# A decoder layer's FFN on one core: the inner layernorm moved behind the second product, its root on GpSimd

## The chip, the core and the metric

The kernel runs on one core of a Trainium2 chip. The core has a matrix engine (TensorE, PE in the profile, with its weight loads shown as PEld), a vector engine (VectorE, DVE), an activation engine (ScalarE, ACT), a general engine (GpSimd, POOL) and a queue engine that issues most DMAs here (SyncE, SP). Each engine works through its own queue in order and waits on semaphores for the others. The metric is the device time of one launch in microseconds. The kernel before took 1366.59 us, the median of three runs (1365.82 to 1367.46).

## The reference

One decoder layer on x of shape (4, 1024, 256): self-attention of 16 heads, cross-attention to 64 context rows, and an FFN with an inner layernorm and ternary weights. Each of the three is added to x.

```python
x = x + attn(layernorm(x), ...)          # 16 heads of 16, 1024 keys
x = x + xattn(layernorm(x), ctx, ...)    # 16 heads of 16, 64 keys
x = x + ffn(layernorm(x), W_fc, ln_w, ln_b, W_proj)

def ffn(x, W_fc, ln_w, ln_b, W_proj):    # 256 -> 1024 -> 256
    h = einsum('btd,hd->bth', x, absmean(W_fc))      # absmean: -1, 0 or 1
    h = gelu(h)
    mu = mean(h, -1); var = mean((h - mu) ** 2, -1)
    h = (h - mu) * rsqrt(var + 1e-5) * ln_w + ln_b
    return einsum('bth,dh->btd', h, absmean(W_proj))
```

The inner layernorm is over the 1024 hidden columns of each token. Its mean and its root are numbers per token, ln_w and ln_b are numbers per hidden column.

## The kernel before

The tokens are worked in four batches of 1024; x lies in three slots of SBUF (`x_slots`) and goes to DRAM and back between the stages (`x_kept`). The program has two parts.

*Attention.* A loop over 16 units (a batch and a group of four heads) runs scores, exponentials and the weighing with v. Generators hang beside it in lines (`due`, `later`, `aside`): the next batch's first layernorm and projections, the batch before's output rows (`post`: the output projection of the self-attention, and the whole cross-attention), and in the last batch the making of the ternary weights (`ternary`) and of one row, `yrow`. That row is the product of ln_b with W_proj; `bias_row` has GpSimd spread ln_b over 128 columns (L764) and TensorE multiply it by the weights in strips of 32 columns, 32 matmuls, and DVE copies the result.

*The last stretch.* What is left when the attention ends is the FFN for all four batches, in eight halves of 512 tokens, and the last batch's `post`. PSUM is divided anew: two tiles of two banks (`wide`) and four of one bank (`misc`). For each half there are two generators.

- `widen(i)`: normalises four token tiles of x (`xn`, DVE, L256), transposes them on TensorE, copies them as a high part `xh` (ScalarE, L269) and a low part `xl` (DVE, L271), has GpSimd add `yrow` to x (L280), and then for each of the four token tiles multiplies by W_fc (eight matmuls of 512 columns: high and low part, two blocks of the width 256, two halves of the 1024 columns), takes Gelu on ScalarE into `h` (L1001) and the statistics on DVE (`bn_stats` L1004, `bn_aggr` L1005). When all four are there, it takes the root on ScalarE (`ln_rstd`: Sqrt L239, reciprocal on DVE L240), the shift `nmr` (DVE L1009), and normalises `h` in place, two tiles on DVE (L1012) and two on ScalarE (L1015).
- `narrow(i)`: for each of the eight blocks c of 128 hidden columns transposes the four token tiles of `h` on TensorE (L60), copies the result times ln_w as a high part `hT` (ScalarE, L1035) and a low part `hl` (DVE, L1036), and two blocks later multiplies both by W_proj into one `wide` tile `py`. At the end DVE adds `py` to x, two token tiles at a time (L1052), and SyncE writes them out.

The order of the work is written by hand. Each generator is cut into pieces by its `yield`s: `widen` into nine, `narrow` into nine. `WIDE` and `NARROW` give each piece a place on a common line of 16 places a half, and the loop at the end takes the piece with the lowest place. Two of every five turns go to a piece of `post` (`turn % 5 in (0, 2)`). A half's Gelu and Sqrt pieces are held back while `post` is between its exponentials (`apart`), and the last two halves wait until `post` is done (`late_x`), since they read its rows. TensorE's and SyncE's instructions keep this order; on the other engines a scheduler orders the instructions as it expects them to be ready, and each engine then keeps to that order.

The bank holds: a `misc` tile is free again when its readers are done; `py` holds one of the two `wide` tiles through a `narrow`, so that a W_fc tile has to wait for the Gelu of the one before it.

Of the kernel before, what the change touches and what calls it, by code (L numbers as in the profile page):

```python
# [8 lines left out]

F32 = mybir.dt.float32  # L10
F32R = mybir.dt.float32r
DRAM = bass.MemoryType.DRAM
AF = mybir.ActivationFunctionType
ALU = mybir.AluOpType
# [6 lines left out]
HID = 1024  # L21
P = 128
# [8 lines left out]
def decoder_layer(ctx, tc, a, out):  # L31
# [151 lines left out]
    def bank():  # L183
        return ps[state["banks"]]()
# [51 lines left out]
    def ln_rstd(pool, rs, mv):  # L236
        n = mv.shape[1]
        sd = pool.tile([P, n], F32, tag="sd", name="sd", bufs=2)
        nc.scalar.activation(sd, mv[:, :, 1], AF.Sqrt, bias=eps_t[:, 0:1])  # L239
        nc.vector.reciprocal(out=rs, in_=sd)  # L240

    def ln_normalised(pool, mv, rs, i, t, n):
        xn = pool.tile([P, n, E], F32, tag="xn", name="xn", bufs=2)
# [473 lines left out]

    ternaries = []

    yrow = const.tile([P, E], F32, name="yrow")  # L720

    def ternary(name, *shape):

# [33 lines left out]
                ALU.is_gt, ALU.subtract,  # L757
            )

    def bias_row():  # L760

        yield "free"
        wide = main.tile([P, HID // P, P], F32, tag="hl", name="lnb_wide", bufs=2)
        nc.gpsimd.tensor_copy(  # L764
            wide, late["lnb"].rearrange("p (c o) -> p c o", o=1).to_broadcast([P, HID // P, P])
        )
        yield "cols"
        pt = bank()
        w = ternaries[1].bitcast(F32)
        product(pt[:, 0:E], [(wide[:, c, :], w[:, c, :]) for c in range(HID // P)])  # L770
        nc.vector.tensor_copy(yrow, pt[:, 0:E])

    def run(gen):
        for _ in gen:
# [116 lines left out]
    for u in range(NU):  # L891
        b, g = divmod(u, NG)
        due.end = aside.end = 2 * NT * NG * (b + 1)
        later.end = due.end - 2
        if b % 2 and g == 0:
            due.end = 2 * NT * (u + 1)
        if g == 0:
            if b == 0:
                later.add(context(), 6)
                later.add(value_bias(), 1)  # L900

            for n in ((1, 2), (), (3,), ())[b]:
                if n > 1:
                    load_x(n)
                due.add(ln1(n), 2)
                due.add(project(n, 0), 8)
                due.add(values(n), 8)
                if n == 1:
                    due.add(project(n, 1), 8)
            if b % 2:  # L910

                due.add(project(b // 2 + 2, 1), 8)
            if b == B - 1:
                load_x(0, view=x_kept, slot=1)
        if g == 1 and b == B - 1:
            aside.add(ternary("wfc", 2, HID), 10)
            aside.add(ternary("wproj", HID // P, E), 10)
            aside.add(bias_row(), 2)
        for step in range(2 * NT):
            half, kb = divmod(step, NT)  # L920
            if step < 2 and u + 1 < NU:
                if step == 0:
                    while pieces_of.get(divmod((u + 1) // 2, NG // 2)) != 4:
                        due.step()
                    fetching = fetch(u + 1)
                next(fetching)
            next(loading, None)
            due.grow(2 * NT * u + step)
            later.grow(2 * NT * u + step)
            aside.grow(2 * NT * u + step)  # L930
            exps = [scores(u, half, kb, 0)]
            top()
            behind = 1 if later.credit >= 1.5 else 0
            if turning and begun[turning[0]] < slots[0]:
                fill("rows", behind)
                run(turning.popleft())
            elif urgent:
                fill("rows", behind)
                urgent.popleft()()
            else:  # L940
                fill("rows", 1)
            exps.append(scores(u, half, kb, 1))

            for _ in range(2 if u == 0 and step < 3 else 1):
                top()
            if pending is not None:
                if pending[2] == 0:
                    acc = ps["acc"]()
                weigh(*pending, acc)
            fill("cols", 2)  # L950
            pending = (u, half, kb, exps)
        if g == NG - 1:

            due.flush()
            aside.flush()
            later.flush()
# [13 lines left out]
    wfc, wproj = ternaries  # L970
    ffn = ctx.enter_context(tc.tile_pool(name="ffn", bufs=1))
    out_view = out.rearrange("(t p) d -> p t d", p=P)
    h_of = {}
    NH = NT // 2

    def widen(i):
        t0 = i * NH
        xh = ffn.tile([P, 2, NH * P], F32R, tag="xh", name="xh", bufs=2)
        xl = ffn.tile([P, 2, NH * P], F32R, tag="xl", name="xl", bufs=2)
        for t in range(0, NH, 2):  # L980
            cols = slice(t * P, (t + 2) * P)
            xn = ln_normalised(ffn, mv3, rs3, t0 + t, t0 + t, 2)
            ln_transposed(xh[:, :, cols], xn, rest=xl[:, :, cols])
            add_row(t0 + t, yrow)
            if t == 0:
                yield ""
        h = ffn.tile([P, NH, HID], F32, tag="h", name="h", bufs=2)
        mv = ffn.tile([P, NH, 2], F32, tag="mvh", name="mvh", bufs=2)
        rs = ffn.tile([P, NH], F32, tag="rsh", name="rsh", bufs=2)
        h_of[i] = h  # L990
        for t in range(NH):
            yield "Gelu"
            ph = ps["wide"]()
            for half in range(2):
                for k in range(4):
                    c, part = divmod(k, 2)
                    matmul(
                        ph[:, half, :], lhsT=(xl, xh)[part][:, c, t * P : (t + 1) * P],
                        rhs=wfc[:, c, half * 512 : (half + 1) * 512], start=k == 0, stop=k == 3,
                    )  # L1000
            nc.scalar.activation(h[:, t, :], ph.rearrange("p a f -> p (a f)"), AF.Gelu)  # L1001
            st = ffn.tile([P, 2, 6], F32, tag="bnh", name="bnh", bufs=3)
            for half in range(2):
                nc.vector.bn_stats(out=st[:, half, :], in_=h[:, t, half * 512 : (half + 1) * 512])  # L1004
            nc.vector.bn_aggr(out=mv[:, t, :], in_=st)  # L1005
        yield "Sqrt"
        ln_rstd(ffn, rs, mv)
        nmr = ffn.tile([P, NH], F32, tag="nmr", name="nmr", bufs=2)
        nc.vector.scalar_tensor_tensor(nmr, mv[:, :, 0], -1.0, rs, ALU.mult, ALU.mult)  # L1009
        for t in range(0, NH, 2):  # L1010
            yield ""
            nc.vector.tensor_scalar(  # L1012
                h[:, t, :], h[:, t, :], mv[:, t, 0:1], rs[:, t : t + 1], ALU.subtract, ALU.mult
            )
            nc.scalar.activation(  # L1015
                h[:, t + 1, :], h[:, t + 1, :], AF.Identity, bias=nmr[:, t + 1 : t + 2],
                scale=rs[:, t + 1 : t + 2],
            )

    def narrow(i):  # L1020


        h = h_of.pop(i)
        t0 = i * NH
        py = ps["wide"]()
        parts = []
        for c in range(HID // P + 2):
# [10 lines left out]
            if c >= 2:  # L1038
                for k, part in enumerate(parts[c - 2]):
                    for n in range(NH):  # L1040


                        matmul(
                            py[:, n // 2, n % 2 * E : (n % 2 + 1) * E], lhsT=part[:, n * P : (n + 1) * P],
                            rhs=wproj[:, c - 2, :], start=c == 2 and k == 0 and n % 2 == 0,
                            stop=c == HID // P + 1 and k == 1 and n % 2 == 1,
                        )
            if 0 < c < HID // P + 1:
                yield ""
        for n in range(2):  # L1050
            rows = xs(t0 + 2 * n, 2)
            nc.vector.tensor_tensor(  # L1052
                rows, rows, py[:, n, :].rearrange("p (n d) -> p n d", n=2), ALU.add
            )
            dma(out=out_view[:, t0 + 2 * n : t0 + 2 * n + 2, :], in_=rows)
        if i == 1:
            load_x(2, view=x_kept, slot=1)

# [15 lines left out]

    WIDE, NARROW = (-6, -4, 0, 1, 3, 7, 8, 10, 12), (2, 4, 5, 6, 9, 11, 13, 14, 15)
    halves = 2 * B
    wides = [Source(widen(i), 16 * i, WIDE) for i in range(halves)]
    narrows = [Source(narrow(i), 16 * (i + 1), NARROW) for i in range(halves)]  # L1080
# [1 line left out]
    tag = later.tag  # L1082
    while tag is not None or narrows:
        turn += 1
        if tag is not None and turn % 5 in (0, 2):
            exps += "Exp" in tag
            tag = next(last, None)
            continue
        sources = []
        if wides:  # L1090
            i = halves - len(wides)
            first = len(wides[0].places) <= len(WIDE) - 2
            late_x = i >= 2 * (B - 1) and tag is not None
            full = first and len(narrows) > halves + 1 - i
            apart = exps % NG and tag is not None and wides[0].tag in ("Gelu", "Sqrt")
            if not (late_x or full or apart):
                sources.append(wides[0])
        if narrows and len(narrows) > len(wides):
# [65 lines left out]
```

## Time and profile before

| what | value |
|---|---|
| median of three runs | 1366.59 us |
| the profiled execution | 1365.17 us |
| its span, first to last instruction | 1363.4 us |
| mean granted TensorE clock | 0.979 |
| TensorE busy in the span | 1282.1 us, 94% |
| VectorE busy | 1004.7 us, 74% |
| ScalarE busy | 898.5 us, 66% |
| GpSimd busy | 80.0 us, 6% |

The last stretch begins at 1102.5 us of the span. At 1281 the last matmul of `post` has run, and from there to 1358.5 TensorE has the FFN alone.

How to read it: a row of a group names the line, the engine, the operation, the tile written and the tiles read, the shapes, the count, then the busy time in all and the mean duration in ns, and behind the bar the idle time of the engine just before and what ended it. The chain of waits is followed back from the last instruction: each piece is the work that the next one waited for. In the busy time by stretch each engine's busy microseconds stand with the count of its instructions, and the granted clock as a share of full speed. A plain matmul on 32-bit floats shows as two records.

### The profile page before, as it was taken

How to read it: one execution, taken by the hardware profiler on the slowest of the kernel's cores; microseconds unless marked ns; L12 is line 12 of the kernel's file. 1: busy time of each engine (PE TensorE's matmuls, PEld its weight loads, DVE VectorE, ACT ScalarE, POOL GpSimd, SP SyncE). 2: the span in 40 equal slices, each digit the busy share in tenths (PEclk: the TensorE clock that was granted, in tenths of full speed). 3: DMA queues.
4: the chain of work that ended last, by engine and by line, in shares of the span. 5: the costliest groups of instructions: out<-in, count | busy, mean ns of one | idle time of the engine just before them, and what ended most of it. 6: DMA issues, size and time to landing. Idle time of an engine off the chain costs nothing.

```text
span 1363.4 us, 27651 instructions
## 1 busy us (share of the span) xinstructions
PE 1282.1 (94%) x11000; PEld 717.4 (53%) x11000; DVE 1004.7 (74%) x2110; ACT 898.5 (66%) x1654; POOL 80.0 (6%) x86
## 2 busy tenths in 40 slices
PE   3879999999999999999999999999999988999987
PEld 1434445545545454444545544545455466776777
DVE  4877777867878877877877777878889357565665
ACT  1377666756687667777676676676766746474765
POOL 4000000003010000011000000010000012000000
PEclk9889999999999999989999999999999989999989
DMA  5440312312130202131212112212210010100000
GB/s 169 126 143 30 111 42 68 94 48 63 41 85 1 63 7 57 33 93 31 64 35 60 38 27 75 82 53 73 55 40 1 2 62 1 44 19 31 1 31 32
DMA packets 46064, 72.72 MB, mean 53 GB/s; under 512 B 11280, under 2 KB 27920, under 8 KB 45936
## 3 DMA queue, kind: packets, MB, share of 16 engines
q1 hardware_dynamic: 44720, 68.47, 17.0%
q8 instruction: 87, 1.43, 0.4%
q10 hardware_dynamic: 1072, 2.10, 0.4%
q0 software_dynamic: 144, 0.39, 0.2%
q14 instruction: 41, 0.34, 0.1%
HBM read 46.81 MB, written 24.12 MB: 52 GB/s over the span
## 4 chain that ended last, share of the span: by engine, by line
PE 73%; DVE 16%; ACT 8%; issue 2%; DMA 1%; SPq 0%; DVEq 0%; ACTq 0%
PE ps_ring L57 42%; PE ps_acc L57 15%; PE ps_wide L57 8%; DVE mx L433 8%; PE ps_misc L57 3%; ACT exp L888 3%; PE ps_misc L60 2%; PE ps_ring L60 2%; DVE nm L592 2%; ACT xn L250 1%; DVE xn L256 1%; DVE bn L233 1%; DMA x<-in_x 1%; ACT ex L625 1%; ACT hl L359 1%
## 5 line engine op out<-in xcount | busy, mean ns | idle before, releaser
L433 DVE TENSOR_REDUCE mx<-ps_ring 128x1 f32<-128x512 f32 x1024 | 646.4, 682 | 157.6 <-PE ps_ring L57 156.7
L888 ACT ACTIVATE exp<-ps_ring 128x512 f32<-128x512 f32 x1024 | 549.2, 606 | 191.1 <-PE ps_ring L57 187.5
L57 PE MATMUL ps_ring<-q,k 64*128 64x512 f32 x1024 | 280.5, 474 | 8.0 <-ACT exp L888 5.9
L57 PE MATMUL ps_ring<-k,q 64*128 64x512 f32 x1024 | 260.2, 425 | 20.1 <-DMA q<-kept_q 7.9
L57 PE MATMUL ps_acc<-exp,v_sb 128*32 128x512 f32 x2048 | 275.3, 610 | 0.0
L57 PE MATMUL ps_ring<-mT,sel 64*128 64x512 f32 x1024 | 232.8, 400 | 0.2 <-ACT mT L451 0.2
L57 PEld LDWEIGHTS ps_ring<-q,k 64*128 64x128 f32 x1024 | 115.5, 185 | 198.4 <-ACT exp L888 69.0
L57 PEld LDWEIGHTS ps_ring<-k,q 64*128 64x128 f32 x1024 | 124.2, 186 | 100.2 <-ACT exp L888 41.3
L57 PEld LDWEIGHTS ps_ring<-mT,sel 64*128 64x128 f32 x1024 | 108.0, 186 | 6.3 <-ACT mT L451 0.7
L57 PEld LDWEIGHTS ps_acc<-exp,v_sb 128*32 128x32 f32 x2048 | 40.5, 108 | 67.4 <-issue 65.6
L1004 DVE BATCH_NORM_STATS2 bnh<-h 128x6 f32<-128x512 f32 x64 | 41.2, 679 | 34.1 <-ACT h L1001 34.0
L1001 ACT ACTIVATE h<-ps_wide 128x1024 f32<-128x1024 f32 x32 | 32.7, 1026 | 41.6 <-PE ps_wide L57 41.5
L1036 DVE SCALAR_TENSOR_TENSOR hl<-ps_misc,lnw,hT 128x512 fp32r<-128x512 f32 x64 | 46.4, 733 | 18.2 <-ACT hT L1035 18.2
L57 PE MATMUL ps_wide<-wproj,hl 128*128 128x256 f32 x256 | 46.2, 303 | 12.6 <-DVE hl L1036 12.5
L57 PE MATMUL ps_wide<-wfc,xl 128*128 128x512 f32 x128 | 56.5, 442 | 1.4 <-DVE xl L271 1.4
L57 PE MATMUL ps_wide<-wfc,xh 128*128 128x512 f32 x128 | 54.3, 424 | 0.0
L1035 ACT ACTIVATE hT<-ps_misc,lnw 128x512 fp32r<-128x512 f32 x64 | 42.6, 687 | 16.3 <-PE ps_misc L60 16.3
L233 DVE BATCH_NORM_STATS2 bn<-x 128x6 f32<-128x256 f32 x96 | 38.8, 416 | 8.1 <-DMA x<-in_x 6.4
L57 PEld LDWEIGHTS ps_wide<-wproj,hl 128*128 128x128 f32 x256 | 34.9, 191 | 16.2 <-DVE hl L1036 14.8
L280 POOL TENSOR_TENSOR x<-x,xbo 128x512 f32<-128x512 f32 x16 | 20.6, 1295 | 367.0 <-ACT xn L250 358.5
L57 PE MATMUL ps_wide<-wproj,hT 128*128 128x256 f32 x256 | 41.4, 284 | 0.0
L407 ACT COPY v_sb<-ps_ring 128x256 f32<-128x256 f32 x32 | 12.0, 375 | 41.0 <-PE ps_ring L57 30.6
(166 smaller groups left out, 1467.1 us busy)
## 6 DMA issues: line engine op xcount, KB each, us to landing
k<-kept_k SPq DMA_DIRECT2D x248, 64.0 KB
q<-kept_q SPq DMA_DIRECT2D x240, 64.0 KB
kept_q<-hl SPq DMA_DIRECT2D x15, 512.0 KB
kept_k<-hl SPq DMA_DIRECT2D x14, 512.0 KB
out<-x SPq DMA_DIRECT2D x16, 256.0 KB
x<-in_x SPq DMA_DIRECT2D x3, 1024.0 KB
x_kept<-x SPq DMA_DIRECT2D x3, 1024.0 KB
x<-x_kept SPq DMA_DIRECT2D x3, 1024.0 KB
```

Of the source, the lines that this page charges most:

```text
L57: ordered(nc.tensor.matmul(*args, **kwargs))
L60: ordered(nc.tensor.transpose(*args))
L233: nc.vector.bn_stats(out=st, in_=xs(t)[:, 0, :])
L250: nc.scalar.activation(xn[:, k, :], xs(t + k)[:, 0, :], AF.Identity, bias=nmr[:, k : k + 1], scale=rs[:, i + k : i + k + 1],)
L280: nc.gpsimd.tensor_tensor(xs(t, 2), xs(t, 2), row.rearrange("p (o d) -> p o d", o=1).to_broadcast([P, 2, E]), ALU.add,)
L433: nc.vector.tensor_reduce(mx[:, t, 2 * pair + n : 2 * pair + n + 1, kh], pm, AX.X, ALU.max)
L592: nc.vector.tensor_reduce(nm[:, t, s, :], pm[s].rearrange("p (h k) -> p h k", k=SK), AX.X, ALU.max, negate=True,)
L888: nc.scalar.activation(ex[:, n, :], pe[n], AF.Exp)
L1001: nc.scalar.activation(h[:, t, :], ph.rearrange("p a f -> p (a f)"), AF.Gelu)
L1004: nc.vector.bn_stats(out=st[:, half, :], in_=h[:, t, half * 512 : (half + 1) * 512])
L1035: nc.scalar.activation(hT, pt, AF.Copy, scale=w)
L1036: nc.vector.scalar_tensor_tensor(hl, pt, w, hT.bitcast(F32), ALU.mult, ALU.subtract)
```

## The change

The inner layernorm is taken through the second product. With r the root and m the mean of a token, (h - m) r ln_w W_proj is r (h ln_w W_proj) - m r (ln_w W_proj). So `narrow` multiplies `h` as it comes from Gelu, and the rest is done on the result's rows:

- `widen` no longer normalises `h`; it ends with the fourth token tile, and has six pieces instead of nine. The root and the shift -m r come from a new function, `ln_root`, on GpSimd: 17 small instructions on 128x4 numbers, a first guess from the bits of the number and three steps of Newton's method.
- A second row, `crow`, the product of ln_w with W_proj, is made as `yrow` is (`rows_of_proj` replaces `bias_row`).
- `narrow` adds crow times the shift to each of the four token tiles of x while it runs, at its blocks 4 and 6 (DVE, 128x256 each), and at its end multiplies `py` by the root and adds it to x, one token tile at a time (four DVE instructions instead of two).
- The places change, and four of every nine turns go to `post`.

```diff
+    def ln_root(pool, rs, mv):
+        n = mv.shape[1]
+        by = pool.tile([P, 4, n], F32, tag="root", name="root", bufs=2)
+        var, half, t, nmr = (by[:, i, :] for i in range(4))
+        engine = nc.gpsimd
+        engine.tensor_scalar(var, mv[:, :, 1], LN_EPS, None, ALU.add)
+        engine.tensor_scalar(half, var, -0.5, None, ALU.mult)
+        engine.tensor_scalar(
+            rs.bitcast(I32), var.bitcast(I32), -0.5, float(0x5F3759DF), ALU.mult, ALU.add
+        )
+        for _ in range(3):
+            engine.tensor_tensor(t, rs, half, ALU.mult)
+            engine.tensor_tensor(t, t, rs, ALU.mult)
+            engine.tensor_scalar(t, t, 1.5, None, ALU.add)
+            engine.tensor_tensor(rs, rs, t, ALU.mult)
+        engine.tensor_tensor(nmr, mv[:, :, 0], rs, ALU.mult)
+        engine.tensor_scalar(nmr, nmr, -1.0, None, ALU.mult)
+        return nmr
...
-    def bias_row():
+    def rows_of_proj():
+        for row, name in ((yrow, "lnb"), (crow, "lnw")):
+            yield "free"
+            wide = main.tile([P, HID // P, P], F32, tag="hl", name=f"{name}_wide", bufs=2)
+            nc.gpsimd.tensor_copy(
+                wide, late[name].rearrange("p (c o) -> p c o", o=1).to_broadcast([P, HID // P, P])
+            )
+            yield "cols"
+            pt = bank()
+            w = ternaries[1].bitcast(F32)
+            product(pt[:, 0:E], [(wide[:, c, :], w[:, c, :]) for c in range(HID // P)])
+            nc.vector.tensor_copy(row, pt[:, 0:E])
...
-            aside.add(bias_row(), 2)
+            aside.add(rows_of_proj(), 4)
...
-        yield "Sqrt"
-        ln_rstd(ffn, rs, mv)
-        nmr = ffn.tile([P, NH], F32, tag="nmr", name="nmr", bufs=2)
-        nc.vector.scalar_tensor_tensor(nmr, mv[:, :, 0], -1.0, rs, ALU.mult, ALU.mult)
-        for t in range(0, NH, 2):
-            yield ""
-            nc.vector.tensor_scalar(
-                h[:, t, :], h[:, t, :], mv[:, t, 0:1], rs[:, t : t + 1], ALU.subtract, ALU.mult
-            )
-            nc.scalar.activation(
-                h[:, t + 1, :], h[:, t + 1, :], AF.Identity, bias=nmr[:, t + 1 : t + 2],
-                scale=rs[:, t + 1 : t + 2],
-            )
+        shift_of[i] = rs, ln_root(ffn, rs, mv)
...
+            if c in (4, 6):
+                for n in range(c - 4, c - 2):
+                    row = xs(t0 + n)[:, 0, :]
+                    nc.vector.scalar_tensor_tensor(row, crow, nmr[:, n : n + 1], row, ALU.mult, ALU.add)
...
-        for n in range(2):
-            rows = xs(t0 + 2 * n, 2)
-            nc.vector.tensor_tensor(
-                rows, rows, py[:, n, :].rearrange("p (n d) -> p n d", n=2), ALU.add
-            )
-            dma(out=out_view[:, t0 + 2 * n : t0 + 2 * n + 2, :], in_=rows)
+        for n in range(NH):
+            row = xs(t0 + n)[:, 0, :]
+            nc.vector.scalar_tensor_tensor(
+                row, py[:, n // 2, n % 2 * E : (n % 2 + 1) * E], rs[:, n : n + 1], row, ALU.mult,
+                ALU.add,
+            )
+            if n % 2:
+                dma(out=out_view[:, t0 + n - 1 : t0 + n + 1, :], in_=xs(t0 + n - 1, 2))
...
-    WIDE, NARROW = (-6, -4, 0, 1, 3, 7, 8, 10, 12), (2, 4, 5, 6, 9, 11, 13, 14, 15)
+    WIDE, NARROW = (-4, -2, 2, 5, 8, 10), (0, 1, 3, 4, 6, 7, 9, 11, 13)
...
-        if tag is not None and turn % 5 in (0, 2):
+        if tag is not None and turn % 9 in (0, 2, 4, 6):
...
-            apart = exps % NG and tag is not None and wides[0].tag in ("Gelu", "Sqrt")
+            apart = exps % NG and tag is not None and wides[0].tag == "Gelu"
```

More of the change, by code (lines that the diff above doesn't have):

```diff
@@ L11 @@
 F32R = mybir.dt.float32r
+I32 = mybir.dt.int32
 DRAM = bass.MemoryType.DRAM
@@ L718, in decoder_layer @@
     ternaries = []
-    yrow = const.tile([P, E], F32, name="yrow")
+    yrow, crow = (const.tile([P, E], F32, name=name) for name in ("yrow", "crow"))
     def ternary(name, *shape):
@@ L758, in ternary @@
             )
-    def bias_row():
[L762 to L765, printed above, removed]
-        )
[L767 to L771, printed above, removed]
+    def rows_of_proj():
[10 more added lines that the diff above has]
+            nc.vector.tensor_copy(row, pt[:, 0:E])
     def run(gen):
@@ L972, in decoder_layer @@
     out_view = out.rearrange("(t p) d -> p t d", p=P)
-    h_of = {}
+    h_of, shift_of = {}, {}
     NH = NT // 2
@@ L1005, in widen @@
             nc.vector.bn_aggr(out=mv[:, t, :], in_=st)
-        yield "Sqrt"
-        ln_rstd(ffn, rs, mv)
-        nmr = ffn.tile([P, NH], F32, tag="nmr", name="nmr", bufs=2)
-        nc.vector.scalar_tensor_tensor(nmr, mv[:, :, 0], -1.0, rs, ALU.mult, ALU.mult)
-        for t in range(0, NH, 2):
-            yield ""
-            nc.vector.tensor_scalar(
-                h[:, t, :], h[:, t, :], mv[:, t, 0:1], rs[:, t : t + 1], ALU.subtract, ALU.mult
-            )
-            nc.scalar.activation(
-                h[:, t + 1, :], h[:, t + 1, :], AF.Identity, bias=nmr[:, t + 1 : t + 2],
-                scale=rs[:, t + 1 : t + 2],
-            )
+        shift_of[i] = rs, ln_root(ffn, rs, mv)
     def narrow(i):
         h = h_of.pop(i)
+        rs, nmr = shift_of.pop(i)
         t0 = i * NH
```

## The prediction

> **What bounds the kernel now.** I read the page first, then the busy time by stretch, the groups of the last stretch, the chain of waits inside it and GpSimd's own rows. The change touches the FFN, which runs in the last 260 us beside the last batch's output rows, so that stretch is read by itself.
>
> ```profile
> span 1363.4 us, 27651 instructions
> PE 1282.1 (94%) x11000; PEld 717.4 (53%) x11000; DVE 1004.7 (74%) x2110; ACT 898.5 (66%) x1654; POOL 80.0 (6%) x86
> ```
>
> ```profile
> 1102.50:1281.00 178.50, 163.56 (x963) 123.59 (x964) 114.39 (x244) 107.33 (x141) 20.79 (x16) 0.96 0.07 23
> 1281.00:1358.50 77.50, 69.75 (x479) 63.12 (x477) 53.54 (x101) 49.62 (x63) 5.35 (x4) 0.96 0.07 21
> 1299.60:1303.10 3.50, 3.50 (x10) 2.73 (x9) 1.93 (x3) 0.51 (x2) 1.86 (x2) 0.51 0.36 120
> ```
>
> The columns are PE, weight load, DVE, ACT, POOL, granted clock, DMA. TensorE is the bound, and it has holes: 23 us without a matmul in the first two stretches together. Behind a hole the clock is granted at 0.51 for 3.4 us, which costs 1.7 us more. It followed holes of 2.24, 2.29, 2.89 and 3.65 us, and did not follow the one of 1.51 us at 1343.5. Hole plus lost clock is the only time to be won, since the change leaves the FFN's products as they are.
>
> ```profile
> L1036 DVE SCALAR_TENSOR_TENSOR hl<-ps_misc,lnw,hT 128x512 fp32r<-128x512 f32 x64 | 46.4, 733 | 18.2 <-ACT hT L1035 18.2
> L1015 ACT ACTIVATE h<-h,nmr,rsh 128x1024 f32<-128x1024 f32 x16 | 19.1, 1233 | 0.5 <-DVE nmr L1009 0.5
> L1001 ACT ACT_TABLE_LOAD x12 | 15.4, 1283 | 4.1 <-PE ps_wide L57 3.9
> L239 ACT ACT_TABLE_LOAD x10 | 12.8, 1283 | 0.2
> L1012 DVE TENSOR_SCALAR h<-h,mvh,rsh 128x1024 f32<-128x1024 f32 x16 | 12.2, 807 | 0.0
> ```
>
> ```profile
> 1315.81 0.69 ACT hT L1035
> 1316.50 0.02 issue
> 1316.52 1.28 ACT L239
> 1317.80 0.01 issue
> 1317.81 0.30 ACT sd L239
> 1318.11 0.48 ACT xh L269
> 1318.58 2.34 ACT h L1015 x2
> 1320.92 0.47 ACT xh L269
> 1321.40 0.02 issue
> 1321.42 0.69 DVE xl L271
> 1322.12 0.67 DVE hl L1036
> ```
>
> One hole, read step by step: ScalarE loads the root's table, takes the root, normalises two tiles, and only then copies xh, which xl and hl wait for; TensorE starts again at 1322.83. Of these 7 us, 3.9 are instructions that the change removes.
>
> **The change, part by part.**
>
> *Removed.* Per half batch of FFN (8 of them): one Sqrt with its reciprocal and its shift, two normalising tiles on DVE and two on ScalarE. ScalarE loses 16 x 1.233 = 19.7 us, 2.4 us of roots, and table loads: by the instruction order 11 stay of 24, so 13 x 1.283 = 16.7 us. DVE loses 16 x 0.807, 16 final adds of 0.683 (L1052), 8 shifts of 0.297 and 8 reciprocals of 0.176: 27.6 us.
>
> *Added on DVE.* 64 scalar_tensor_tensor of 128x256, half with crow, half from the second product. The nearest rows are bo (L535, 0.425 us) and hl in strips (L360, 0.484): 27.2 to 31.0 us. DVE's load thus stays; it is hidden by the 88 us that DVE is idle before 1358.5, and what matters is where in its queue the new work stands.
>
> *The second row, crow.* 32 more matmuls of 32 columns behind the attention. The chain has the like of them (yrow's, 64 records) at 3.45 us, in a stretch where PE is busy 48.6 of 50 us: +3.5 us, nothing covers it. The bounds are 0 (if filled into a hole) and 3.6.
>
> *Holes that go.* Those whose chain holds removed instructions, each with its lost clock: 1128 (two L1012 before xl) 1.0; 1221 to 1235 (L239 1.28, L1015 2.26) 1.4; 1273 (L239 before ao) 1.4; 1298 4.2; 1323 4.6; 1343 to 1348 2.3. Sum -14.9 us. Others go by the new order: 1139 to 1142.6 (hl behind six xn of 3.97 us) 5.3, since a wfc tile of 1.87 us and eight transposes of 0.87 now stand between; the xl wait at 1106.7, filled with att's transposes, 0.7; three waits of ao, hl and xn2T at 1122.7, 1135.9, 1150.2, 2.3: -8.3 us. At 1199 attx keeps PE 2.3 us; eight h transposes (0.87) now precede it, the hole falls to 1.4 and the clock is kept: -2.6 us.
>
> *The wait that is new.* Two things on DVE stand between the last Gelu of a half and its first hl. From the end of the last wfc tile: Gelu 1.03, two bn_stats 1.27, xl 0.63, aggregate 0.1, four final rows 4 x 0.425, xl 0.63, hl 0.70: hl is ready at 6.15 us. PE has until then two wproj pieces of 0.95, two transposes of xn of 0.44 and twelve of h (1.31): 4.1 us. So each seam in the FFN-only part has a hole of 2.1 us, twice, and the last half 1.4 + 0.5: +6.1 us. With the post pieces between, the first seam comes out at 3.1 and loses its clock (+4.8), and three later ones are half covered (+3.2).
>
> *Order and end.* Per half the FFN had 18 pieces beside two post pieces in three, now 15 beside four in five: 12 either way, so the post rows keep their place and get nothing in the sum. The output DMAs stay as many, each behind two final rows; after the last product stand four rows of 0.425 instead of two of 0.683: +0.3 us.
>
> *The root on GpSimd.* 17 steps, each waiting on the one before, with yrow's adds queued behind them; crow's rows wait for the last, and behind them in DVE's queue stand hl and, at the second seam, the maxima nm that free kx's banks.
>
> ```profile
> L463 POOL COPY xwq<-xwq_in 128x64 f32<-128x64 f32 x8 | 1.5, 240 | 16.9 <-DMA xwq_in<-in_xwq 16.9
> L280 POOL TENSOR_TENSOR x<-x,yrow 128x512 f32<-128x512 f32 x16 | 20.8, 1302 | 213.2 <-DVE xn L256 142.8 <-issue 67.9 <-DVE rsh L240 2.3
> ```
>
> No row shows a 128x4 step there. The low end is a 128x1 memset (0.100), the high end the copy of 128x64 (0.240) plus the 0.23 that POOL idled between two adds that waited on DVE: 0.47. I take 0.24: 4.1 us a root, 1.7 to 8.0. In the FFN-only seam crow stands third behind hl, and its delay reaches PE only past 5.35 us (0.31 a step). At the second seam an add of 1.3 us stands in the root's queue, 5.4 us in all: DVE waits 1.6 us, +1.6.
>
> A page of the Trainium skill speaks against this part: "GPSIMD Engine Reference", section "Engine selection", says that elementwise work with two inputs belongs on VectorE, GpSimd being about twice slower. Twice the DVE row of a 128x4 step (0.154) would be 0.31 us a step, 5.2 us a root, just under the point where it costs. No run here shows it yet; the sum would gain about 2 us.
>
> The same page's table in "Specifications" says that DVE's two-port and two-input instructions contend with GpSimd for SBUF. The trace agrees: xn (L256) takes 0.38 us alone and 0.66 in the run of six beside POOL's adds. Crow's rows read two SBUF tensors; beside steps of four columns I price that at nothing, at most 32 x 0.28 = 9 us of DVE time, mostly in its idle time.
>
> **Sum.** +3.5 - 14.9 - 8.3 - 2.6 + 6.1 + 4.8 + 3.2 + 0.3 + 1.6 = -6.3 us. The profiled execution took 1365.17 us (span 1363.4); its like would be 1358.9. The median of the runs is 1.4 higher: 1360.3 us.
>
> **The rivals.**
>
> *The clock.* My seam's hole of 2.1 us lies between the 1.51 that kept the clock and the 2.24 that lost it. If the five further seams each lose 1.7, +8.5 us: 1368.8. For it: four holes of that size did; against: PE's fillers at the seams are underrated by the time of one transpose.
>
> *GpSimd's chain ends late (the other side).* At 0.47 us a step a root takes 8.0 us. Past my 4.1 that is 3.9 us at each of the first two seams, 2.65 at the two FFN-only seams, 3.4 in the last half and half of 2.65 at three: about +20, 1380 us. It decides from 0.33 us a step, where 1.5 us at some five seams eats the 6.3. For it: each step waits on its own engine's semaphore; against: the copy's eight ran in 1.5 us.
>
> *The seams are covered.* If post pieces and a short root (1.7 us) leave nothing at the seams but the FFN-only ones and 1 us: +3.5 - 14.9 - 8.3 - 2.6 + 6.1 + 1 = -15.2, 1351.4.
>
> *It does not do what it says:* the holes are due to DVE's order, and each removed wait has its like behind it. Then only crow's product is left: 1370.
>
> **How the numbers follow.** The sum's own case, 1354 to 1364: 0.40. Seams covered, 1344 to 1354: 0.22. Clock lost, 1364 to 1371: 0.18. Late root or no gain, above 1370: 0.20. With a tenth or a little less left out at each end the range is 1345 to 1376. Less than 0.2% (2.7 us) can't be told from no change: faster 0.61, same 0.12, slower 0.27.
>
> **What would show it.** Right: in the last stretch no table load of L239's kind for mvh, ACT 35 us less busy; the chain at the last two seams running bn_stats, final rows, hl, with holes near 2.1 us; GpSimd's steps near 0.24 us. Wrong: DVE idle before crow's rows with GpSimd as releaser (the late root), the clock at 0.5 behind every seam, or holes of the old size with another releaser. A different order on DVE than the times assume would upset the seam's sum most.

## The result, and the profile after

The changed kernel took 1373.72 us, the median of seven runs (1368.84 to 1374.56), against 1366.59 us before (seven runs by then, 1364.57 to 1367.46). The ratio is 1.0051, with a 95% interval of 1.0037 to 1.0064: slower, by 7 us, where 6.3 us less had been forecast. The profiled execution is the shortest of the seven, 1368.84 us with a span of 1367.1 us, 3.7 us above that of before.

The page of the changed kernel, its first and its busy lines:

```profile
span 1367.1 us, 27909 instructions
PE 1280.9 (94%) x11064; PEld 717.8 (53%) x11064; DVE 1007.2 (74%) x2127; ACT 861.0 (63%) x1617; POOL 109.6 (8%) x223
```

ScalarE is busy 37.5 us less (35 were forecast), VectorE as long as before, and TensorE too: what was to be won was holes, and the question is which holes there are now. The busy time by stretch (PE, weight load, DVE, ACT, POOL, granted clock, DMA), for the last stretch up to 1281 us, its remainder, and two stretches of 7 us inside it:

```profile
1106.10:1281.00 174.90, 157.46 (x928) 119.10 (x928) 111.11 (x236) 81.61 (x116) 35.39 (x84) 0.94 0.07 24
1281.00:1362.00 81.00, 74.94 (x512) 67.95 (x512) 59.49 (x123) 37.91 (x53) 19.51 (x72) 0.98 0.06 20
1165.00:1172.00 7.00, 6.13 (x25) 5.04 (x26) 5.84 (x10) 2.06 (x3) 0.00 (x0) 0.52 0.23 77
1243.00:1250.00 7.00, 5.23 (x22) 4.75 (x23) 6.00 (x14) 1.96 (x3) 0.36 (x1) 0.55 0.23 75
```

The second line is nearly the FFN-only part (the last batch's rows end 6 us into it); it got a better clock than before, 0.98 where it had 0.96. The part beside the last batch's rows (first line) has 17.4 us without a matmul where before had 14.9, and a clock of 0.94 for 0.96. In the two short stretches TensorE runs at about half its clock, for 6.8 us each.

The groups that were shown of before, and those that take their place:

```profile
L1051 DVE SCALAR_TENSOR_TENSOR hl<-ps_misc,lnw,hT 128x512 fp32r<-128x512 f32 x64 | 46.2, 735 | 10.3 <-ACT hT L1050 10.0
L1066 DVE SCALAR_TENSOR_TENSOR x<-crow,root,x 128x256 f32<-128x256 f32 x32 | 14.1, 476 | 16.1 <-POOL root L262 16.1
L1071 DVE SCALAR_TENSOR_TENSOR x<-ps_wide,rsh,x 128x256 f32<-128x256 f32 x32 | 13.2, 471 | 4.5 <-PE ps_wide L58 4.5
L1026 ACT ACT_TABLE_LOAD x6 | 7.7, 1283 | 1.6 <-PE ps_wide L58 1.5
L240 ACT ACT_TABLE_LOAD x3 | 3.8, 1283 | 0.1
L259 POOL TENSOR_SCALAR root<-root 128x4 f32<-128x4 f32 x24 | 5.4, 224 | 2.1
L257 POOL TENSOR_TENSOR root<-rsh,root 128x4 f32<-128x4 f32 x24 | 4.9, 203 | 1.8
```

The second line carries the result: crow's rows (L1066) make VectorE stand for 16.1 us, always for the last step of the root on GpSimd (L262). It waits at eight places; three of them, 2.55, 3.06 and 2.35 us, stand ahead of large holes in TensorE's work. The waits, which engine and line waited for which, with the sum, the count and the longest in us, show what that does to TensorE:

```profile
DVE x L1066 <- POOL root L262: 16.1, 8, 3.1
PE ps_wide L58 <- DVE hl L1051: 9.4, 5, 3.5
PE ps_misc L58 <- DVE nm L615: 4.0, 1, 4.0
PE ps_misc L61 <- DVE nm L615: 3.4, 1, 3.4
```

Three holes of 3.4 to 4.0 us are among them. The chain of waits into the second one, start and duration in us, with most of the root's like steps left out (here and in the chains below also the pieces called `issue`, each of at most 0.08 us):

```profile
1154.36 1.04 ACT h L1026
1155.42 1.30 DVE bnh L1029 x2
1156.74 0.22 DVE mvh L1030
1157.04 0.24 POOL root L251
...
1161.44 1.21 POOL x L303
1162.65 0.17 POOL root L261
...
1162.90 0.24 POOL root L262
1163.16 0.48 DVE x L1066
1163.65 1.57 DVE x L1071 x4
1165.22 0.61 DVE nm L615
1165.87 2.07 PE ps_misc L58 x6
```

Read from the top: the statistics of the next half are ready at 1156.96, the root takes from 1157.04 to 1163.14 with one of yrow's adds (L303) ahead of its last two steps, and VectorE waits with a row of crow at the head of its queue. That row belongs to the half whose statistics have just been taken; in the program it stands inside that half's `narrow`, at block 4, behind the hl of blocks 0 to 4. On VectorE it stands ahead of the four final rows (L1071) of the half before and ahead of the maxima nm (L615) of the cross-attention, and TensorE waits for the first of these nm for 3.96 us. The other two big holes have the same shape: at 1132.41 one row of crow and hl behind it (hole 3.46), at 1243.60 one row of crow, four final rows, two nm (hole 3.44).

Adding up the last stretch, from the first transposes behind the attention's last product to the last matmul, gives this. Holes are the time in which the trace has no matmul there; the clock's loss is half the time at half speed outside the holes; the rest is TensorE's own work.

| kernel | last stretch | holes | of these over 3 us | clock's loss | rest |
|---|---|---|---|---|---|
| before | 253.5 | 20.6 | 3.6 | 9.9 | 223.0 |
| before, second profile | 253.2 | 20.8 | 3.6 | 8.9 | 223.5 |
| after | 253.4 | 21.4 | 10.9 | 10.4 | 221.6 |
| after, second profile (`again`) | 254.7 | 21.1 | 10.8 | 12.3 | 221.3 |

So the last stretch did not get shorter (0.1 us less in the first profiles, 1.5 more in the second ones), and it begins 3.6 us later (4.3 in the second ones). That is near the 3.45 us of crow's product, but the attention ahead of it did not run at the same clock in all four profiles, so that leaving the product out, below, is the better measure of it.

### The profile page after: what moved, and what is told of

It reads as the page before. It is cut to its first block, busy times and chain, and to the rows that moved or that the text cites. A ratio compares the mean times of both kernels' runs of the same rounds, so it can differ in the third digit from the quotient of the medians.

```text
span 1367.1 us, 27909 instructions
## 1 busy us (share of the span) xinstructions
PE 1280.9 (94%) x11064; PEld 717.8 (53%) x11064; DVE 1007.2 (74%) x2127; ACT 861.0 (63%) x1617; POOL 109.6 (8%) x223
## 4 chain that ended last, share of the span: by engine, by line
PE 72%; DVE 14%; ACT 7%; DMA 3%; issue 2%; POOL 1%; SPq 1%; ACTq 0%; DVEq 0%; POOLq 0%
PE ps_ring L58 42%; PE ps_acc L58 15%; PE ps_wide L58 8%; DVE mx L456 7%; ACT exp L913 3%; PE ps_misc L58 3%; PE ps_ring L61 2%; DVE nm L615 2%; PE ps_misc L61 2%; DMA x<-in_x 2%; ACT xn L273 1%; DVE bnh L1029 1%; SPq L64 1%; ACT h L1026 1%; DVE x L1071 1%
## 5 line engine op out<-in xcount | busy, mean ns | idle before, releaser
L58 PE MATMUL ps_ring<-q,k 64*128 64x512 f32 x1024 | 281.1, 473 | 10.4 <-ACT exp L913 5.9
L58 PE MATMUL ps_ring<-k,q 64*128 64x512 f32 x1024 | 259.9, 424 | 21.1 <-DMA k<-kept_k 8.1
L303 POOL TENSOR_TENSOR x<-x,xbo 128x512 f32<-128x512 f32 x16 | 20.6, 1295 | 366.5 <-ACT xn L273 358.6
L61 PE MATMUL ps_misc<-ident,h 128*128 128x128 f32 x256 | 39.5, 287 | 5.1 <-DVE nm L615 3.4
L58 PEld LDWEIGHTS ps_wide<-wproj,hl 128*128 128x128 f32 x256 | 36.0, 196 | 12.8 <-DVE hl L1051 10.8
```

Of the source, the lines that this page charges most:

```text
L58: ordered(nc.tensor.matmul(*args, **kwargs))
L61: ordered(nc.tensor.transpose(*args))
L303: nc.gpsimd.tensor_tensor(xs(t, 2), xs(t, 2), row.rearrange("p (o d) -> p o d", o=1).to_broadcast([P, 2, E]), ALU.add,)
```

## Experiments

The theory at this point, called Q (the queue): nothing but the place of crow's rows in VectorE's order makes the loss, since they wait at its head for a root that another engine has not finished. The rivals: the other parts of the change carry it (the second product, the share of turns given to the last batch's rows, called O in part of the texts on record), or GpSimd's small steps cost by their sheer work beside VectorE.

**The changed kernel again.** Nothing is edited; the kernel before was measured beside it.

> The changed kernel once more, nothing edited, for a second profile. Its first profile (1368.8 us) was the shortest of its runs, the median 1373.7. Theory Q (the loss is made where VectorE stands before crow's rows until GpSimd has the root, with the half clock behind): the same three holes of 3.4 to 4.0 us at the seams of the first, second and fourth half, and the 5 us between the two times are one to three more stretches of half clock, at 1.7 to 3.4 us each, behind holes that are near the limit. Rival A (the attention takes longer in most runs, through its loads): the last stretch keeps its 260 us and starts later than at 1106.

It took 1372.64 us (1369.91 to 1374.43), ratio 1.0047 (1.0032 to 1.0063), with the same three holes of 3.44, 3.93 and 3.40 us, each with 6.8 us at half clock, which begin while the hole lasts at the first two and 0.3 us behind it at the third. The attention's stretch had windows of half clock at 586 and 1050 us that the first profile lacks; the profiled execution took 1373.60 us.

**Crow's rows behind hl.** They are kept in the order of the program on VectorE; no instruction is added or removed. The scheduler, given that, also moved other instructions in the last stretch: on VectorE some hl, xn and statistics, on ScalarE two roots of x's layernorms with their table loads. TensorE's and GpSimd's orders stay as they were.

```diff
-                    nc.vector.scalar_tensor_tensor(row, crow, nmr[:, n : n + 1], row, ALU.mult, ALU.add)
+                    ordered(
+                        nc.vector.scalar_tensor_tensor(row, crow, nmr[:, n : n + 1], row, ALU.mult, ALU.add)
+                    )
```

> Crow's rows are kept behind the hl of their own block (blocks 4 and 6) in VectorE's queue; nothing else is edited. Theory Q: VectorE's idle time before crow's rows with GpSimd as releaser falls from 16.1 us to under 2, the holes of 3.5, 4.0 and 3.4 us shrink by 2 to 3 us each and at least two of the three half clocks (3.4 us each) go: 10 to 16 us less than the changed kernel, 1358 to 1364, below the kernel before. Rival R (crow's product and VectorE's own work are the loss; a hole only moves): within 2 us of the changed kernel, holes of the same sum with another releaser.

It took 1356.04 us (1354.74 to 1358.47), ratio 0.9931 (0.9910 to 0.9952): faster than both kernels, with the same 17 steps on GpSimd. The group of crow's rows in this kernel:

```profile
L1067 DVE SCALAR_TENSOR_TENSOR x<-crow,root,x 128x256 f32<-128x256 f32 x32 | 13.9, 476 | 0.0
```

The idle time behind the bar went from 16.1 us to none. At the second seam the chain of waits of this kernel now reads:

```profile
1159.38 1.57 DVE x L1073 x4
1160.95 1.19 DVE nm L615 x2
1162.14 0.60 DVE xl L294
1162.74 1.20 DVE nm L615 x2
1163.94 0.32 DVE xn L279
1164.26 0.67 DVE hl L1051
1164.97 1.22 PE ps_wide L58 x8
```

From 1156.74 on VectorE is busy throughout, the final rows begin at 1159.38, 3.2 us after the statistics of the next half (1156.23; 6.7 us in the kernel above), and the hole before hl's product is 0.78 us. And in the whole last stretch up to 1281 us:

```profile
1108.80:1281.00 172.20, 162.03 (x987) 124.00 (x988) 115.70 (x257) 87.07 (x123) 39.14 (x102) 0.98 0.07 25
```

The granted clock is 0.98 for 0.94. The last stretch took 240.0 us: holes 13.1, clock's loss 5.1. Since no work changed, the order is the cause: it is worth 16 to 17 us by the medians, of which the profiles show 13 to 15 in the last stretch. That it is the place of crow's rows, and not of the others that moved with them, rests on the holes that went, which are the ones behind these rows, and on the runs with a longer and a shorter root below.

**The same again, on another chip.**

> The kernel with crow's rows pinned behind the last hl of their own half, a second time and in more rounds, beside the two that follow. If the order on DVE is the cause, it lands where it did: 1354 to 1359 us, a ratio of 0.991 to 0.996 to the kernel before, with no wait of crow's rows for the root on GpSimd and no hole above 2.1 us behind nm or hl. If the first measurement owed its gain to its few runs or to its chip, it comes out at 1360 to 1364 us, where the two pinned variants of the other chip lay.

1356.79 us (1356.53 to 1358.52), ratio 0.9937 (0.9924 to 0.9949), last stretch 239.6 us, holes 13.1. The gain holds.

**The root longer and shorter.** Six steps of Newton's method for three, in the changed kernel as it is; then one for three.

```diff
-        for _ in range(3):
+        for _ in range(6):
```

> Six steps of Newton's method instead of three: 12 more GpSimd instructions of 0.29 us a half, 3.5 us a root. Theory Q: each of the three holes and the last half's grow by about 3.5 us, the two seams of the FFN alone by 1 to 2: 12 to 18 us more than the changed kernel. Rival R: the root is hidden, no more than 3 us.

1386.07 us (1385.59 to 1386.6), ratio 1.0149 (1.0130 to 1.0167). The waits of this kernel:

```profile
DVE x L1066 <- POOL root L262: 37.1, 8, 6.5
PE ps_wide L58 <- DVE hl L1051: 19.7, 8, 6.9
PE ps_misc L58 <- DVE nm L615: 7.4, 1, 7.4
```

The longest wait of crow's rows grows from 3.1 to 6.5 us, by 3.4; twelve steps of 0.288 us are 3.5. The holes at the first two seams go to 6.9 and 7.4 us, and one of 4.1 us is new in the last half. At the third (1240 in the changed kernel) the expectation failed, and in a telling way: with a longer root the scheduler put crow's rows behind the nm and two hl there,

```profile
1255.97 2.29 DVE L1066 SCALAR_TENSOR_TENSOR x<-crow,root,x 128x256 f32<-128x256 f32 x3 [0.68 <-POOL root L262]
```

and the holes of 3.44 and 1.17 us fell to 0.91 and 1.52, though the root took 3.5 us longer.

```diff
-        for _ in range(3):
+        for _ in range(1):
```

> The changed kernel with one Newton step in place of three, the order untouched. Eight instructions of 0.288 us are gone from each root, so 2.3 us. The wait of crow's rows for the root at the three seams, 3.0 us now, should fall to about 0.7, and the three holes in PE from 3.4 to 3.9 us to 1.1 to 1.6. If those holes are the cause, that gives 3 x 2.3 = 6.9 us, and up to 3 x 3.4 us more if the stretches of half clock behind them go too: 1356 to 1366 us against 1372.6 of the changed kernel. If the root's length is only a part of the chain (the rows' place in the queue costs as much without it), the gain is under 3 us: above 1369.5 us. The root is less exact with one step.

1363.60 us (1360.77 to 1366.45), ratio 0.9986 (0.9975 to 0.9996). The waits:

```profile
DVE x L1066 <- POOL root L262: 3.7, 3, 1.8
PE ps_wide L58 <- DVE hl L1051: 9.0, 6, 1.9
PE ps_misc L58 <- DVE nm L615: 1.3, 1, 1.3
```

No hole of over 3 us is left, though the longest wait is 1.8 us where 0.7 was expected. The ratios 0.9986, 1.0047 and 1.0149 at one, three and six steps lie near a line: 4.2 us for each of the first two steps, 4.6 for each of the last three. One step lengthens a root by 4 x 0.288 = 1.15 us. In the last stretch the holes are 17.3, 21.4 and 33.9 us at one, three and six steps, and the clock's loss 6.4, 10.4 and 12.1 us; since the scheduler moved crow's rows at some seams in both variants, the line is not the sum of the same three holes. With one step the kernel is still 6.8 us slower than the pinned one that was measured beside it.

**The short root in the pinned kernel.**

> The pinned kernel with one Newton step in place of three. Where nothing waits for the root the length of it costs nothing: within 2 us of the pinned kernel of this call. If GpSimd's instructions slow VectorE beside them, or if the wait is only shifted to a place that the chain does not name, two thirds fewer steps give 3 to 6 us.

1357.89 us (1355.71 to 1360.89), ratio 0.9942 (0.9927 to 0.9957), against 0.9937: no difference. Where the rows stand behind hl, the root's length costs nothing that these runs can tell, and eight of its 17 small instructions fewer save nothing.

**Without the second product.** In the changed kernel crow is a copy of yrow: the kernel leaves out the 32 matmuls, and with them the right term of the mean.

```diff
-        for row, name in ((yrow, "lnb"), (crow, "lnw")):
+        for row, name in ((yrow, "lnb"), (crow, None)):
+            if name is None:
+                nc.vector.tensor_copy(row, yrow)
+                return
```

> Crow's product is left out: crow is a copy of yrow (so the mean's term is wrong), which takes away 32 matmuls, one spread on GpSimd and nothing in the last stretch. Both theories: 3.5 us less than the changed kernel, as the chain has 3.45 us for the like. If it gives much less, the attention's end had room for it; if it gives the whole 7 us, the last stretch costs nothing.

1367.74 us (1364.75 to 1371.84), ratio 1.0018 (1.0003 to 1.0034). Against the changed kernel, measured beside it, that is 0.0029, so 4.0 us by the ratios and 4.9 by the medians, about the 3.45 us that the chain shows for the product. The last stretch keeps its holes, 21.1 us. The product explains a good half of the loss to the kernel before, as priced, and none of the distance to the pinned kernel.

**The kernel before, once more.**

> The kernel before once more, nothing edited, for a second profile. In the changed kernel's later profiles the attention has a half clock at about 586 us and one at 1050 that its first profile does not have. Theory C (the attention's half clocks come and go in every kernel): a span within 2 us of 1363.4 with half clocks at other places in the attention. Rival A (they belong to the change): the half clock at 579 and 593 as in the first profile, nothing at 586 or 1050.

1367.63 us in a single run, span 1365.9. In its last stretch holes and clock stand as in the first profile (the table above); the windows of half clock ahead of it lie elsewhere (588 for 579 and 593).

**The root back on ScalarE, rows pinned.** The root is taken by `ln_rstd` again, and the shift by VectorE.

```diff
-        shift_of[i] = rs, ln_root(ffn, rs, mv)
+        ln_rstd(ffn, rs, mv)
+        nmr = ffn.tile([P, NH], F32, tag="nmr", name="nmr", bufs=2)
+        nc.vector.scalar_tensor_tensor(nmr, mv[:, :, 0], -1.0, rs, ALU.mult, ALU.mult)
+        shift_of[i] = rs, nmr
```

> On top of crow_pinned: the root goes back to ScalarE (Sqrt with its table load, the reciprocal and the shift on VectorE), while the layernorm stays behind the second product and crow's rows behind their block's hl. Theory T (with the wait gone, the gain over the kernel before is ScalarE's freed queue, table loads included): 13 more table loads of 1.28 us, some of which stand before hT at the seams: 4 to 9 us more than crow_pinned, so 1360 to 1365. Rival N (ScalarE has room at the seams, the gain is the normalising alone): within 2 us of crow_pinned.

1362.42 us (1360.18 to 1364.17), ratio 0.9981 (0.9972 to 0.9990): by the ratios 6 to 7 us slower than the pinned kernel. The table loads of this kernel in the last stretch:

```profile
L1026 ACT ACT_TABLE_LOAD x11 | 14.1, 1283 | 2.5 <-PE ps_wide L58 2.4
L240 ACT ACT_TABLE_LOAD x9 | 11.5, 1283 | 0.2
```

With three of the exponentials' they are 23 for 12. Holes are 15.7 us for 13.1, the clock's loss 8.0 for 5.1. With the rows pinned, the root on GpSimd is thus worth its place.

**The old share of turns, rows pinned.**

```diff
-        if tag is not None and turn % 9 in (0, 2, 4, 6):
+        if tag is not None and turn % 5 in (0, 2):
```

> On top of crow_pinned: two of five turns for the last batch's rows, as before the change, in place of four of nine. By the count of pieces both give 12 post pieces a half at most (15 x 2/3 = 10 against 15 x 4/5 = 12), so post ends later and less FFN is left behind it: theory P (the ratio matters little once no wait stands in VectorE's queue): within 3 us of crow_pinned. Rival O (the ratio carries a good part of the gain): 4 us or more slower.

1362.72 us (1360.34 to 1364.96), ratio 0.9982 (0.9970 to 0.9993), 6 to 7 us slower than the pinned kernel: holes 15.0 us, clock's loss 8.7. With the rows pinned the share of four in nine is a gain; in the changed kernel as it is the old share was not tried, but nothing here speaks for its carrying the loss.

**The final rows later, rows pinned.** The final rows of three halves are issued behind the next half's first three hl, and kept in that order on VectorE by `ordered` (not shown in the cut below).

```diff
+            if c == 2 and ends:
+                ends.popleft()()
...
-        for n in range(NH):
-            row = xs(t0 + n)[:, 0, :]
+        def end():
+            for n in range(NH):
+                row = rows_of[n]
...
+        if i in FIN:
+            ends.append(end)
+        else:
+            end()
+    FIN = (4, 5, 6)
```

> On top of crow_pinned: the four final rows of the halves 4, 5 and 6 are issued behind the first three hl of the next half instead of before them. Theory S (the 1.85 us holes at the last seams are hl waiting behind those rows, as the sum of the prediction has it: 1.7 us): the three holes of 1.85, 1.85 and 1.54 us fall under 0.8 each, and the half clock at the first goes: 4 to 6 us less than crow_pinned, about 1351. Rival B (the second wide tile of PSUM is freed by those rows, and TensorE then waits for it): holes of the same size with the final rows as releaser, within 1.5 us.

1357.99 us (1357.26 to 1358.33), ratio 0.9952 (0.9937 to 0.9967): no gain. The timeline of TensorE in this kernel at the first of the two FFN-only seams, the time waited and its releaser in brackets:

```profile
1295.51 0.75 PE L58 MATMUL ps_wide<-wproj,hl 128*128 128x256 f32 x4 [0.93 <-DVE hl L1052]
1296.09 0.64 PE L58 MATMUL ps_wide<-wproj,hT 128*128 128x256 f32 x4
1298.39 0.49 PE L58 MATMUL ps_wide<-wfc,xl 128*128 128x512 f32 x1 [1.66 <-DVE x L1079]
```

The wait for hl falls from 1.85 to 0.93 us, and 1.66 us appear 3 us later: `py` holds one of the two `wide` tiles until the final rows have read it, and the next W_fc tile waits for them. At the second of these seams it is 0.75 and 1.68 us. In the last half, behind which no W_fc tile follows, the hole does fall, from 1.54 to 0.69 us. In the whole last stretch there are 13.6 us of holes for 13.1: at the two seams the wait changed its place and was not saved.

## Why the prediction was wrong

*Holes that go: right.* None of the holes that it named with the root's and the normalising's lines is left. At attx 0.85 us remain (1.4 forecast) and the clock is kept there. Some were priced too high: counted as time without a matmul and clock lost behind it, the 25.8 us of the sum are nearer 23 in the profile before (between 1221 and 1235, priced at 1.4, it has 0.1).

*Crow's product: right.* The chain of the changed kernel has it at 3.45 us, and leaving it out gave 4.0.

```profile
1100.98 3.45 PE ps_ring L58 x64
```

*The FFN-only seams: right.* The chain of the first one in the changed kernel:

```profile
1301.60 1.04 ACT h L1026
1302.67 1.29 DVE bnh L1029 x2
...
1304.66 1.52 DVE x L1071 x4
1306.18 0.60 DVE xl L294
1306.78 0.67 DVE hl L1051
1307.49 4.61 PE ps_wide L58 x16
```

It is the order that was worked out, with holes of 1.86, 1.86 and 1.54 + 0.69 us for 2.1, 2.1 and 1.4 + 0.5 (the items of its list for VectorE add up to 6.06 us and not to the 6.15 written there). No row of crow and no root is in it: crow stands behind the first hl here, and the root's 4.85 us (1304.75 to 1309.60) stay under the 5.35 us of the prediction. Half clock followed one of the two equal holes, 1.7 us that the sum did not have.

*VectorE's added work: right.* The 64 rows take 14.1 + 13.2 = 27.3 us (27.2 to 31.0 forecast), and the mean hl is no slower, 0.735 us for 0.733. ScalarE's items add up to 38.8 us less and not to the 35 of its sign; it was 37.5, with 12 table loads in the last stretch for the 11 expected.

*A step on GpSimd: nearly.* Busy 0.20 to 0.25 us in the mean of each kind, start to start 0.288 us, a root 4.85 us where no add stands in it; the prediction took 0.24 and 4.1, inside its bounds. The rule it weighed, in the Trainium skill, "GPSIMD Engine Reference", section "Engine selection" (two-input elementwise work about twice slower there than on VectorE, one-input work about level), shows no such split at four columns: the step with two tensors took 0.203 us, the one with one tensor 0.224, against the 0.154 us of a 128x4 step on VectorE.

*Where crow's rows stand: the step that failed.* "At the second seam an add of 1.3 us stands in the root's queue, 5.4 us in all: DVE waits 1.6 us, +1.6" names the right wait at the right place, and even the nm behind it. What it cost was 3.06 us of wait, a hole of 3.96 us, and 3.1 us of clock, which the sum left out. And it priced one seam of three. The first seam ("+4.8") and the three later ones ("half covered (+3.2)") were worked out from a list without a row of crow ahead of hl, as it is in the FFN-only part; the traces show it ahead of hl at 1132 and ahead of four final rows and nm at 1243. Measured, the three seams are 3.46 + 3.96 + 3.44 + 1.17 = 12.0 us of holes and 2.8 + 3.1 + 2.8 = 8.7 us of clock, 20.7 us in place of 4.8 + 1.6 + 3.2 = 9.6. These 11.1 us more, less 1.4 us by which TensorE's own time there fell (no run shows why), eat the 9.8 us that the last stretch should have lost (-6.3 without the product's 3.5). The other terms cancel, with some luck: the FFN-only seams cost 1.5 us more than forecast, and 1.3 us more went elsewhere, where a window of half clock at the start of the stretch, about 3 us of loss before and none in the first profile after, was in no term. That the engine orders were fixed by a scheduler, by its own estimate of when a root is ready, was known; only the order in the FFN-only part and at the second seam was written out in the sum. The prediction did name the risk in its last lines ("A different order on DVE than the times assume would upset the seam's sum most") and the sign that came ("DVE idle before crow's rows with GpSimd as releaser"); it gave neither a term in the sum.

*The rivals.* The late chain on GpSimd was the right one in kind, but "decides from 0.33 us a step" was wrong: it decided at 0.288 us a step, since at three seams crow's rows stood ahead of the work for TensorE, where the sum had the root covered for its first 4.1 us. "It does not do what it says", 1370 us, came nearest in time and not in its cause, since the removed waits did not come back in other places; a new one came. In the pinned kernel's first profile the three seams keep 4.5 us of holes and 1.7 of clock, and its 1356 to 1357 us stand where the prediction's own case did (1354 to 1364).

*What stays open.* The profiled pairs differ by 3.7 us (first profiles) and 5.9 (second ones), the medians by 7. The runs of one kernel lie up to 7 us apart. Behind the first 100 us, which are alike, the windows of half clock ahead of the last stretch cost nothing in the first profile of the changed kernel and 5.1 us in the second, and 3.4 us in each of the two of before; without them the pairs would differ by 7.1 and 4.2 us. Why they come and go was not tried. Nor is it known where the 2 to 3 us lie that the pinned kernel gains, by the medians, beyond what its last stretch shows.

## What to carry to other kernels

An instruction that waits for another engine's long chain costs what stands behind it in its own queue, so before pricing the chain, write out what follows that instruction at every place where it occurs, in the order of the engine and not of the program. If the order is a scheduler's, a cheap test is to pin the one instruction behind the work that feeds the bottleneck: here one line turned +7 us into -9. And a hole's price includes the clock that is lost behind it, here 8.7 us on 12.0 us of holes.

## What the runs showed of the hardware

A chain of dependent GpSimd instructions on 128x4 numbers advances by 0.288 us a step (the median in the changed kernel): about 0.21 us of work and 0.07 between the end of one and the start of the next. The means of the single steps lie between 0.200 and 0.250 us, those with two tensors (0.200 to 0.205) a little below those with one (0.212 to 0.250).

Windows of half clock are 3.4 us long or multiples of that in these traces. The length does not follow from the hole alone: 6.8 us went with each of the three holes of 3.4 to 4.0 us in both profiles of the changed kernel, and 10.2 with one of 7.4 in the kernel with the long root, but a hole of 4.1 us there was followed by 3.4, and the one of 3.65 in the kernel before by 3.4 in one profile and by 6.8 in the other. The Trainium skill, "TensorE: Matmul & The Clock Gate", Part 1, gives the same unit, and says that the clock falls after an idle window of about 3.4 us. The runs here agree with the unit and not with that bound: a hole of 1.85 us was followed by 3.4 us at half clock in the pinned kernel at 1298, and not at 1321 behind one of the same length.
